# Softplus's last addition as an accumulating transfer issued by GpSimd, in a two-layer metaformer kernel

## The chip, the cores and the metric

The kernel runs on one core of a Trainium2 chip. The metric is the device time of one execution in microseconds. The time before is 26,376.83 us, the median of three runs that lie between 26,376.42 and 26,384.82.

## The reference

Input and output are 8 images of 128 x 128 tokens with 96 channels. Layer 0 mixes tokens with a filter in the Fourier domain and then applies a feed-forward block in 8-bit floats. Layer 1, which takes most of the time and holds the change, mixes tokens with a selective scan over 16,384 tokens in both directions:

```python
xc = silu(depthwise_conv3x3(xc) + conv_b)            # 192 channels
delta = jax.nn.softplus(dts + dt_projs_bias)          # step size of each channel and token
dA = jnp.exp(delta[..., None] * As)                   # 16 states for each channel
h = dA * h + (delta * u)[..., None] * Bt[:, :, None, :]
y = jnp.sum(h * Ct[:, :, None, :], axis=-1)
out = (y_forward + y_backward + skip) * silu(z) @ W_out.T
```

The kernel computes Softplus from the absolute value and the positive part of its argument a: with e = exp(-|a|) and w = 1 + e it takes log(w), corrects it for the digits of e that were lost in the sum, and adds max(a, 0).

## The kernel before

**Layer 0** fills the first 5,300 us and is not touched by the change. **The scan layer** works through 4 pairs of images. For each pair there are 32 jobs: 16 chunks of 1,024 tokens forward (`d == 0`), then the same chunks backward (`d == 1`), 128 jobs in all. A job has 12 blocks of 32 channels, and a block has 4 units of 4 states each. So a unit is one tile of 128 partitions (32 channels x 4 states) by 1,024 tokens, and a job has 48 units.

The order of the work is written out by hand. Every step is given to a `Plan` with a time in units (one unit is one scan), the plan is sorted by time, and the instructions are emitted in that order. Each engine executes its own instructions in that order, one after the other; waits come from the tiles that instructions share. A job's 48 units take about 164 us, a unit about 3.4 us.

For one unit these steps follow each other:

- SyncE loads `dlb` (step sizes spread over the states, L1209), `bt` (L1193) and `ct` (L1200) from DRAM. `dlb` and `bt` have 3 buffers, `ct` has 5.
- ScalarE makes `da`, the decay, in PSUM (L1235, two buffers).
- TensorE spreads `du` = delta x u over the states into `dub` in PSUM (L1222, `spread`, one buffer, once a block).
- VectorE multiplies `bt` by `dub` into `hp` (L1252, two units at a time) and scans in place (L1287). In some forward blocks GpSimd makes one of these products from `dus`, ScalarE's copy of `dub` (L1271).
- ScalarE keeps the last state for the next chunk (L1296).
- GpSimd multiplies the scanned states by `ct` into `hc` (L1303, three buffers).
- TensorE sums `hc` over the states into `y` (L1312).

Backward jobs also multiply by the gate (`yo`, L1368, GpSimd) and run the output projection (`po`, L1442 and L1446, TensorE) and the feed-forward block in steps laid between the units (`finish_steps`). Forward jobs have the taps of the 3 x 3 convolution on TensorE instead (`pv`, L1035).

**Softplus** is made one job ahead, in `prepare_steps`, three times a job: one chain for each of three tiles of 128 channels, in the order tile 0, tile 2, tile 1, called the first, second and third chain here. A chain runs: TensorE projects (`pd`, L1116); ScalarE takes the absolute value into `e` (L1125) and the positive part into `rl` (L1126), then exp (L1129), 1 + e into `w` (L1133) and log (L1136); VectorE computes what was lost (L1139); GpSimd subtracts it from `w` (L1144), adds `rl` to `w` (L1147) and multiplies `w` by `u` into `du` (L1154); SyncE stores `w` to `dld` in DRAM (L1150), from where `dlb` is loaded in the next job. `e`, `rl` and `w` have one buffer each. The planned times of the GpSimd and SyncE steps in a chain are set here:

```python
PREP = tuple(
    {
        "delta": (a0, a1), "exp": e, "onep": e + 0.2, "lost": e + 1.5, "log": e + 2.2,
        "sub": s0, "add": s1, "mul": m, "store": s1 + 1.1,
    }
    for a0, a1, e, s0, s1, m in (
        (12.2, 13.2, 16.2, 20.3, 21.3, 24.3),
        (24.2, 25.2, 28.2, 32.3, 33.3, 36.3),
        (37.2, 38.2, 41.2, 45.3, 48.3, 49.3),
    )
)
```

In the first two chains the addition is planned 3 units before the product with `u`, in the third chain 1 unit before it. The third chain's addition and product fall at the start of the job that follows.

Of the kernel before, what the change touches and what calls it, by code (L numbers as in the profile page):

```python
# [14 lines left out]
ALU = mybir.AluOpType  # L15
# [886 lines left out]
def scan_layer(tc, p, x2d, xcd, zsd, ud, yfd, dld, bcd, out):  # L902
# [7 lines left out]
    nc = tc.nc  # L910
# [3 lines left out]
    with ExitStack() as ctx:  # L914
# [87 lines left out]
        def halves():  # L1002
            return [(i, slice(i * HALF, (i + 1) * HALF)) for i in range(2)]

        def kind(t):
            return 0 if t < 2 else 1
# [74 lines left out]
        def prepare_steps(plan, bp, d, c, k, at0):  # L1081


            k.u, k.du = [None] * 3, [None] * 3

            def load(t):
                k.u[t] = w1.tile([128, TC], F32, tag=f"u{t}", name="u")
                nc.sync.dma_start(k.u[t], ud[bp % 2, t, :, c * TC : (c + 1) * TC])

            def project(i, hs):  # L1090
                def f():
                    if i == 0:
                        k.bc = w1.tile([NX, TC], F32, tag="bc", name="bc")
                    px = ps1.tile([NX, HALF], F32, tag="pp", name="px")
                    for t in range(3):
                        nc.tensor.matmul(  # L1096
                            px, xpw[:, d, t, :], k.u[t][:, hs], start=(t == 0), stop=(t == 2)
                        )
                    k.px = px

                return f

            def projected(hs):
                nc.scalar.copy(k.bc[:, hs], k.px)

            def store_bc():
                nc.sync.dma_start(bcd[k.s], k.bc[0 : 4 * NST])


            def delta(t, st, i, hs):  # L1110
                def f():
                    if i == 0:
                        st["e"] = w1.tile([128, TC], F32, tag="e", name="e")
                        st["r"] = w1.tile([128, TC], F32, tag="rl", name="rl")
                    pd = ps1.tile([128, HALF], F32, tag="pp", name="pd")
                    nc.tensor.matmul(  # L1116
                        pd, dtw[4 * NST : NX, d, t, :], k.bc[4 * NST : NX, hs], start=True, stop=True
                    )
                    st["pd"] = pd

                return f

            def parts(t, st, hs):
                bias = dtb[:, d, kind(t) : kind(t) + 1]
                nc.scalar.activation(st["e"][:, hs], st["pd"], AF.Abs, bias=bias)  # L1125
                nc.scalar.activation(st["r"][:, hs], st["pd"], AF.Relu, bias=bias)  # L1126

            def exp(st):
                nc.scalar.activation(st["e"], st["e"], AF.Exp, scale=-1.0)  # L1129

            def onep(st):
                st["w"] = w1.tile([128, TC], F32, tag="w", name="w")
                nc.scalar.activation(st["w"], st["e"], AF.Copy, bias=1.0)  # L1133

            def log(st):
                nc.scalar.activation(st["w"], st["w"], AF.Ln)  # L1136

            def lost(st):
                nc.vector.scalar_tensor_tensor(  # L1139
                    st["e"], st["w"], -1.0, st["e"], ALU.add, ALU.subtract  # L1140
                )

            def sub(st):
                nc.gpsimd.tensor_tensor(st["w"], st["w"], st["e"], ALU.subtract)  # L1144

            def add(st):
                nc.gpsimd.tensor_tensor(st["w"], st["w"], st["r"], ALU.add)  # L1147

            def store(t, st):
                nc.sync.dma_start(dld[k.s, t], st["w"])  # L1150

            def mul(t, st):
                k.du[t] = w1.tile([128, TC], F32, tag=f"du{t}", name="du")
                nc.gpsimd.tensor_tensor(k.du[t], st["w"], k.u[t], ALU.mult)  # L1154

            for t, at in ((0, 0.4), (1, 3.2), (2, 4.2)):
                plan(at0 + at, lambda t=t: load(t))
            for i, hs in halves():
                plan(at0 + 9.2 + 1.3 * i, project(i, hs))
                plan(at0 + 10.2 + 1.1 * i, lambda hs=hs: projected(hs))  # L1160
            plan(at0 + 12, store_bc)
            for t, at in ((0, PREP[0]), (2, PREP[1]), (1, PREP[2])):
                st = {}
                for i, hs in halves():
                    plan(at0 + at["delta"][i], delta(t, st, i, hs))
                    plan(at0 + at["delta"][i] + 0.6, lambda t=t, st=st, hs=hs: parts(t, st, hs))
                for what, f in (
                    ("exp", exp), ("onep", onep), ("lost", lost), ("log", log), ("sub", sub),
                    ("add", add),
                ):  # L1170
                    plan(at0 + at[what], lambda f=f, st=st: f(st))
                plan(at0 + at["mul"], lambda t=t, st=st: mul(t, st))
                plan(at0 + at["store"], lambda t=t, st=st: store(t, st))
# [640 lines left out]
```

## Time and profile before

| what | value |
|---|---|
| median of three runs | 26,376.83 us |
| the profiled execution | 26,377.52 us |
| its span, first to last instruction | 26,375.7 us |
| mean granted TensorE clock | 0.914 |
| VectorE busy | 25,019.3 us |
| GpSimd busy | 22,505.7 us |
| TensorE busy | 22,322.2 us |
| ScalarE busy | 17,618.2 us |
| SyncE's transfer queue, share of 16 engines | 41.7%, 3,496 MB |
| transfers issued by GpSimd | none |

The profile comes from one execution. A group is all instructions of one line, engine, operation and pair of tiles; it has a busy time, a mean duration, and the idle time that its engine had just before it, with the instruction that ended most of that idle time. A timeline lists one engine's instructions by start time and merges neighbours of a kind (x2, x3). In it PE is TensorE, DVE is VectorE, ACT is ScalarE, POOL is GpSimd and SP is SyncE; `<-` means written from, or, after an idle time, released by. The time of a transfer "to landing" runs from its issue to the signal that all its data are there.

### The profile page before, as it was taken

How to read it: one execution, taken by the hardware profiler on the slowest of the kernel's cores; microseconds unless marked ns; L12 is line 12 of the kernel's file. 1: busy time of each engine (PE TensorE's matmuls, PEld its weight loads, DVE VectorE, ACT ScalarE, POOL GpSimd, SP SyncE). 2: the span in 40 equal slices, each digit the busy share in tenths (PEclk: the TensorE clock that was granted, in tenths of full speed). 3: DMA queues.
4: the chain of work that ended last, by engine and by line, in shares of the span. 5: the costliest groups of instructions: out<-in, count | busy, mean ns of one | idle time of the engine just before them, and what ended most of it. 6: DMA issues, size and time to landing. Idle time of an engine off the chain costs nothing.

```text
span 26375.7 us, 272252 instructions
## 1 busy us (share of the span) xinstructions
PE 22322.2 (85%) x84560; PEld 8957.9 (34%) x84560; DVE 25019.3 (95%) x18514; ACT 17618.2 (67%) x31776; POOL 22505.7 (85%) x13815
## 2 busy tenths in 40 slices
PE   8999999889997777899977778998777788877777
PEld 6777777622222222222222222222222222212222
DVE  5888888699999999999999999999999999999999
ACT  5888887556666666666666666666666666656666
POOL 3666666489999999999999999999999999999998
PEclk9999999999998888999988889999888899988888
DMA  2333333344444444444444444444444444444443
GB/s 61 94 94 95 94 92 89 86 154 154 155 159 136 136 136 139 148 158 156 155 139 135 138 135 155 154 153 154 140 137 137 136 151 155 153 144 135 135 139 114
DMA packets 1887106, 3513.56 MB, mean 133 GB/s; under 512 B 564382, under 2 KB 999190, under 8 KB 1885626
## 3 DMA queue, kind: packets, MB, share of 16 engines
q1 hardware_dynamic: 1885652, 3496.14, 41.7%
q8 instruction: 672, 11.01, 0.2%
q14 instruction: 782, 6.41, 0.1%
HBM read 2739.32 MB, written 756.17 MB: 133 GB/s over the span
## 4 chain that ended last, share of the span: by engine, by line
DVE 41%; PE 18%; issue 15%; ACT 4%; POOL 3%; DVEq 0%; DMA 0%; POOLq 0%; ACTq 0%
DVE hp L1287 22%; DVE hp L1252 17%; PE pv L1035 6%; PE dub L1222 5%; PE y L1312 5%; POOL hc L1303 2%; DVE e L1139 2%; ACT da L1235 1%; PE y L1354 1%; PE pd L1116 1%; PE px L1096 0%; ACT pre L1049 0%; ACT L1061 0%; ACT L1060 0%; ACT ff_h L1543 0%
## 5 line engine op out<-in xcount | busy, mean ns | idle before, releaser
L1303 POOL TENSOR_TENSOR hc<-hp,ct 128x1024 f32<-128x1024 f32 x6144 | 14732.5, 2418 | 1175.4 <-DVE hp L1287 1048.3
L1287 DVE TENSOR_TENSOR_SCAN hp<-da,h,hp 128x1024 f32<-128x1024 f32 x6144 | 14143.0, 2338 | 207.3 <-ACT da L1235 49.0
L1312 PE MATMUL y<-hc,sely 128*32 128x512 f32 x24576 | 6959.0, 651 | 2061.1 <-POOL hc L1303 2045.0
L1235 ACT ACTIVATE da<-dlb,at 128x1024 f32<-128x1024 f32 x6144 | 6844.8, 1114 | 0.5 <-ACT h L1296 0.5
L1252 DVE TENSOR_TENSOR hp<-bt,dub 128x2048 f32<-128x2048 f32 (+1 forms) x3072 | 6558.2, 2135 | 13.4 <-PE dub L1222 12.9
L1222 PE MATMUL dub<-du,selx 128*128 128x512 f32 x6144 | 3800.0, 751 | 1332.0 <-DVE hp L1252 1331.7
L1296 ACT COPY h<-hp 128x1 f32<-128x1 f32 x6144 | 1159.1, 189 | 4769.7 <-DVE hp L1287 4753.4
L1035 PE MATMUL pv<-xin,cdiag 128*128 128x512 f32 x6912 | 3495.5, 625 | 113.8 <-ACT pre L1049 52.2
L1312 PEld LDWEIGHTS y<-hc,sely 128*32 128x32 f32 x24576 | 938.8, 112 | 6575.8 <-POOL hc L1303 4361.2
L1222 PEld LDWEIGHTS dub<-du,selx 128*128 128x128 f32 x6144 | 1286.0, 226 | 3478.7 <-issue 2164.0
L1035 PEld LDWEIGHTS pv<-xin,cdiag 128*128 128x128 f32 x6912 | 1174.5, 190 | 2466.2 <-issue 2066.4
L110 POOL TENSOR_SCALAR ln_v<-ln_v 128x4 f32<-128x4 f32 x768 | 199.9, 260 | 1288.0 <-DVE ln_v L106 1267.9
L1271 POOL TENSOR_TENSOR hp<-bt,dus 128x1024 f32<-128x1024 f32 x366 | 867.4, 2370 | 254.7 <-ACT dus L1264 204.4
L1049 ACT ACTIVATE pre<-pv,cbt 128x512 f32<-128x512 f32 x384 | 263.8, 687 | 1102.0 <-PE pv L1035 914.1
L1116 PE MATMUL pd<-bc,dtw 12*128 12x512 f32 x1536 | 913.4, 675 | 67.7 <-ACT rl L1126 47.0
L1144 POOL TENSOR_TENSOR w<-w,e 128x1024 f32<-128x1024 f32 x384 | 904.7, 2356 | 51.7 <-ACT w L1136 38.2
L111 POOL TENSOR_TENSOR ln_r<-ln_v,mhalf 128x4 f32<-128x4 f32 x768 | 885.7, 1153 | 64.0
L1154 POOL TENSOR_TENSOR du<-w,u 128x1024 f32<-128x1024 f32 x384 | 908.9, 2367 | 0.2
L1147 POOL TENSOR_TENSOR w<-w,rl 128x1024 f32<-128x1024 f32 x384 | 906.6, 2361 | 0.2
L1125 ACT ACTIVATE e<-pd,dtb 128x512 f32<-128x512 f32 x768 | 524.9, 683 | 549.5 <-PE pd L1116 532.9
L742 PE MATMUL ring<-xnt,win 96*128 96x512 f32 x1536 | 782.3, 617 | 70.8 <-ACT xnt L736 69.8
L1096 PE MATMUL px<-u,xpw 128*76 128x512 f32 x1536 | 717.2, 603 | 59.8 <-ACT ff_h L1536 57.5
(189 smaller groups left out, 32947.9 us busy)
## 6 DMA issues: line engine op xcount, KB each, us to landing
dlb<-dld SPq DMA_DIRECT2D x1536, 512.0 KB, 5.2
bt<-bcd SPq DMA_DIRECT2D x1024, 512.0 KB, 4.7
ct<-bcd SPq DMA_DIRECT2D x1024, 512.0 KB, 4.7
u<-ud SPq DMA_DIRECT2D x384, 512.0 KB, 5.0
dld<-w SPq DMA_DIRECT2D x384, 512.0 KB, 3.5
ud<-pre SPq DMA_DIRECT2D x192, 512.0 KB, 4.2
yf<-ud SPq DMA_DIRECT2D x768, 128.0 KB, 4.8
yfd<-yo SPq DMA_DIRECT2D x384, 256.0 KB, 7.1
```

What stands on the lines that cost most here:

```text
L1035: nc.tensor.matmul(st["pv"], cdiag[:, kind(t), j, :], st["xin"][:, r : r + HB // 2, j % 3 : j % 3 + W], start=(j == 0), stop=(j == 8),)
L1116: nc.tensor.matmul(pd, dtw[4 * NST : NX, d, t, :], k.bc[4 * NST : NX, hs], start=True, stop=True)
L1144: nc.gpsimd.tensor_tensor(st["w"], st["w"], st["e"], ALU.subtract)
L1147: nc.gpsimd.tensor_tensor(st["w"], st["w"], st["r"], ALU.add)
L1154: nc.gpsimd.tensor_tensor(k.du[t], st["w"], k.u[t], ALU.mult)
L1222: nc.tensor.matmul(blk["du"][:, hs], selx[:, blk["r"], :], k.du[blk["t"]][:, hs], start=True, stop=True,)
L1235: nc.scalar.activation(un["da"], blk["dl"], AF.Exp, scale=at[:, d, blk["kb"], j : j + 1])
L1252: nc.vector.tensor_tensor(hp[:, 0:n, :], bt[blk["b2"], j][:, 0:n, :], blk["du"].rearrange("p (o t) -> p o t", o=1).to_broadcast([128, n, TC]),
L1287: nc.vector.tensor_tensor_scan(h, da, h, un["init"], op0=ALU.mult, op1=ALU.add)
L1296: nc.scalar.copy(un["init"], un["h"][:, last : last + 1])
L1303: nc.gpsimd.tensor_tensor(un["hc"], un["h"], ct[blk["b2"], j], ALU.mult)
L1312: nc.tensor.matmul(y[q, :], sely, un["hc"][:, hs], start=False, stop=(j == NG - 1),)
```

## The change

In Softplus's step `add`, GpSimd's addition of two tiles in SBUF is replaced by a transfer that GpSimd issues. The transfer reads the tile `r` (named `rl` in the profile) and adds it to `w` in place, 128 partitions x 1,024 floats, 512 KB. It stands in the plan where the addition stood. The step runs 384 times, three for each of 128 jobs.

```diff
             def add(st):
-                nc.gpsimd.tensor_tensor(st["w"], st["w"], st["r"], ALU.add)
+                nc.gpsimd.dma_start(st["w"], st["r"], accum_op=ALU.add)
```

Against the instruction order before, the order of every engine is the same but for this instruction. The waits differ: the product with `u` (L1154, GpSimd), the store of `w` (L1150, SyncE) and the next writing of `rl` (L1126, ScalarE) wait for the transfer's landing, where they waited for GpSimd's addition. The transfer itself waits for the subtraction (L1144), as the addition did.

## Prediction

> **What bounds the kernel now.** I read the page's busy table first, then busy time by stretch, then the costliest groups, then timelines of one job. The page's first two parts:
>
> ```profile
> PE 22322.2 (85%) x84560; PEld 8957.9 (34%) x84560; DVE 25019.3 (95%) x18514; ACT 17618.2 (67%) x31776; POOL 22505.7 (85%) x13815
> ...
> DVE  5888888699999999999999999999999999999999
> ```
>
> From the seventh slice on (the scan layer, 5,300 us to the end) VectorE is the digit 9 everywhere. The busy time by stretch gives the exact share in mid-kernel:
>
> ```profile
> 10000.00:15000.00 5000.00, 4193.24 (x12052) 1236.04 (x12050) 4950.99 (x2291) 3248.28 (x5535) 4639.74 (x2365) 0.90 0.45 146
> ```
>
> VectorE works 4,951 of 5,000 us (third number with a count), GpSimd 4,640, and the DMA engines are 45% busy. So VectorE is the bound, at 99%; GpSimd has 360 us free in 5,000. Three groups of the page matter:
>
> ```profile
> L1303 POOL TENSOR_TENSOR hc<-hp,ct 128x1024 f32<-128x1024 f32 x6144 | 14732.5, 2418 | 1175.4 <-DVE hp L1287 1048.3
> L1287 DVE TENSOR_TENSOR_SCAN hp<-da,h,hp 128x1024 f32<-128x1024 f32 x6144 | 14143.0, 2338 | 207.3 <-ACT da L1235 49.0
> ...
> L1147 POOL TENSOR_TENSOR w<-w,rl 128x1024 f32<-128x1024 f32 x384 | 906.6, 2361 | 0.2
> ```
>
> The scan waited 207 us in all and never on GpSimd; GpSimd's products `hc` waited 1,048 us on the scan. The third line is the addition that the change replaces: 906.6 us, 2,361 ns each (busy and mean stand after the bar, then the idle time before). Taking work off GpSimd can therefore give VectorE almost nothing. What can go wrong is a new wait on GpSimd that reaches VectorE, so the question is how much delay each chain stands. The tightest place is the third Softplus of a job (tile 1) when the running job is a backward one. GpSimd's timeline there:
>
> ```profile
> 10073.23 2.38 POOL L1147 TENSOR_TENSOR w<-w,rl 128x1024 f32<-128x1024 f32 x1
> 10075.54 2.37 POOL L1303 TENSOR_TENSOR hc<-hp,ct 128x1024 f32<-128x1024 f32 x1
> 10077.85 2.38 POOL L1154 TENSOR_TENSOR du<-w,u 128x1024 f32<-128x1024 f32 x1
> 10080.17 2.36 POOL L1303 TENSOR_TENSOR hc<-hp,ct 128x1024 f32<-128x1024 f32 x1
> 10082.48 1.29 POOL L1368 TENSOR_TENSOR yo<-yo,zs 128x512 f32<-128x512 f32 x1
> 10083.71 4.68 POOL L1303 TENSOR_TENSOR hc<-hp,ct 128x1024 f32<-128x1024 f32 x2
> ```
>
> Only one `hc` stands between the addition and the product that needs it; all six run back to back. TensorE, same job:
>
> ```profile
> 10086.12 1.92 PE L1312 MATMUL y<-hc,sely 128*32 128x512 f32 x4 [1.60 <-POOL hc L1303]
> 10087.97 1.66 PE L1442 MATMUL po<-x,ident 128*128 128x388 f32 x2
> 10089.43 2.45 PE L1446 MATMUL po<-wo,yo 128*128 128x194 f32 x12
> 10091.80 1.05 PE L1312 MATMUL y<-hc,sely 128*32 128x512 f32 x4
> 10092.78 1.98 PE L1222 MATMUL dub<-du,selx 128*128 128x512 f32 x4
> ```
>
> and the VectorE product that reads `dub`:
>
> ```profile
> 10095.89 2.26 DVE L1252 TENSOR_TENSOR hp<-bt,dub 128x2048 f32<-128x2048 f32 x1
> ```
>
> `dub` is ready at 10,094.76 and wanted at 10,095.89: 1.1 us to spare behind an unbroken chain from the `hc` that ends at 10,086.05.
>
> **What the Trainium skill says.** "DMA: Bandwidth & Descriptors", section "SWDGE vs HWDGE vs iDMA": an accumulating transfer must be issued by GpSimd, whose cores write the descriptors in software. No transfer here is GpSimd's yet, so the trace can't confirm it. "Perfetto Trace Analysis", section "DMA Instruction — SWDGE (GPSIMD)": GpSimd is through when the descriptors are written, and the data land later; so its next products run meanwhile, and only the instruction that waits for the landing stands. "Collectives: The Full Stack", section "The bandwidth ceiling: the fold count and why AG ≠ RS ≠ AR": an add in the DMA path costs two source reads and so about half the copy rate, the add itself nothing. No run shows it yet. "SBUF — State Buffer", section "SBUF: two separate sides": a VectorE instruction on the shared port keeps GpSimd from writing descriptors. In the scan VectorE reads one operand from PSUM (`da`, `dub`) and one from SBUF, except L1139 (384 of 1.2 us), which does share: its mean is 1,393 ns against a minimum of 1,198.
>
> **The change part by part.**
>
> *Removed:* 384 additions of 2,361 ns on GpSimd = 907 us. They lie beside VectorE's work; value 0. The bounds: VectorE's port conflicts on L1139 are 384 x (1.393 - 1.198) = 75 us at most, and the additions don't meet L1139, so I take 0 and keep a few us below nothing.
>
> *Added on GpSimd:* 384 issues. Between 0 (a dispatch) and 2.36 us (as the addition) each; I take 1.0, the skill's first-byte latency for GpSimd's transfers ("DMA: Bandwidth & Descriptors", "Latency and other measured facts"). Up to 2.36 us it moves nothing else.
>
> *Added: the landing, L,* counted from where the addition began. All later readers of `w`, and the next writer of `rl`, wait for it. Built up: a 512 KB store of the same tile by SyncE lands after 3.5 us (`dld<-w`, DMA issues). The queue row (3,496 MB in 41.7% of 16 engines' 26,375.7 us) makes 512 KB 1.65 us of all engines; the second source read adds that: 5.15. The skill's first bytes (1.0 us for GpSimd, 0.6 for SyncE) add 0.4: 5.5. In the third chain SyncE has just issued a `u` and a `dlb` load (10,071.55 and 10,072.23), 3.3 us of engine time, about half of which is still open when GpSimd's transfer starts: +1.6. L = 7.1 us, an estimate. Low: 2.0 + 2 x 524,288/436e3 = 4.4 (the fit in the skill's "Anatomy of one DMA — SWDGE (gpsimd) path", two passes). High: two whole transfers of the slowest 512 KB row (`dlb<-dld`, 5.2), one after the other, + 0.4 = 10.8.
>
> *Third chain, 128 times.* The product L1154 began 4.62 us after the addition (10,077.85 - 10,073.23). It now begins at L, and everything behind it on GpSimd slips by L - 4.62: `yo` and three `hc`, then TensorE's `y`, the projection and `dub`. In 64 backward jobs 1.1 us is free, so VectorE loses L - 5.7: 1.4 us x 64 = 90 us. In 64 forward jobs TensorE is full of convolution taps and `dub` is 3.3 us early (ready 11,082.1, read 11,085.46), so loss begins at L = 7.9: 0 now.
>
> *First and second chain, 256 times.* Three `hc` lie between, the product is 9.25 us after the addition:
>
> ```profile
> 10144.97 2.36 POOL L1147 TENSOR_TENSOR w<-w,rl 128x1024 f32<-128x1024 f32 x1
> 10147.27 7.01 POOL L1303 TENSOR_TENSOR hc<-hp,ct 128x1024 f32<-128x1024 f32 x3
> 10154.22 2.37 POOL L1154 TENSOR_TENSOR du<-w,u 128x1024 f32<-128x1024 f32 x1
> ```
>
> At 7.1 nothing; without that cover it would be (7.1 - 2.4) x 256 = 1,200 us of GpSimd delay.
>
> *ScalarE:* L1126 rewrites `rl` 9.8 us after the first chain's addition began (10,154.80), 12 and more after the others. Behind it stand the decays L1235 that the scan needs. Covered until L = 9.8.
>
> *SyncE:* the store L1150 waits for the landing in place of the addition, 4.7 us longer; queued behind it are loads of `ct`, `bt`, `dlb`. Tightest: the first chain's `ct`, used 13 us or more after its issue, landing in 4.7, and issued 2.3 us after the store anyway: 10.6 us of cover. The stored `dld` is read over 18 units (3.4 us each) later.
>
> *DMA engines:* 384 x 3.3 us = 1,267 us, 45% to about 51% busy in the scan: 0.
>
> *Start:* three chains before the first scan, where VectorE waits 12.9 us for `dub` anyway: 0 to 5 us, I take 0.
>
> Sum: the profiled execution took 26,377.5 us (span 26,375.7 and 1.8 around it), 0.7 above the median of 26,376.8. 26,377 + 90 = **26,467 us**, +0.34%.
>
> **The rivals.** *The landing is hidden (not slower).* Place: the third chain's product; price 0 at L of 5.7 or less, 51 us at 6.5. For it: the build-up without collision gives 5.5, the skill's fit 4.4. Against: the two loads in flight. 26,377 to 26,428; it decides below L = 6.5. *A slow transfer.* Descriptors written slowly or a slow add, with L beyond 10.8: at L = 15, 64 x 9.3 + 64 x 7.1, and the first two chains lose too (slack behind 9.25 about 1.6 and 2.8 us: 128 x 4.1 + 128 x 2.9), together 1,950: 28,330. For it: nothing in the trace prices an accumulate. Against: the half-rate statement. *Freed GpSimd pays.* At most the 75 us of port conflicts and the 49 us of waits on `da`: 26,253; against it, GpSimd isn't what VectorE waits for. That the transfer does not do the addition is excluded by the instruction order: it stands in the addition's place on GpSimd, with the same readers.
>
> **How the numbers follow.** About 0.2% (53 us) is what a measurement of this kernel can tell from no change. Forecast (L from 6.5 to 10.8): 0.46. Hidden: 0.34. Slow transfer: 0.16. Freed GpSimd: 0.04. Faster 0.04, same 0.34, slower 0.62. Range: low 26,365 (hidden, a few us gained); high L = 10.8: 64 x 5.1 + 64 x 2.9 = 512, 26,890. The slow transfer (0.16) and most of the gain are left out.
>
> **What would show it.** Right: L1154 begins about 7 us after the issue in the third chain and stays near 9 in the others; VectorE waits 1 to 2 us on `dub` once in each backward job, nowhere in forward ones; SyncE's store waits longer; nobody waits on `rl`. Wrong: L1154 late in all three chains, or ScalarE standing at L1126 (slow transfer); or `hc` slower while descriptors are written; or no new wait at all (hidden).

## The result and the profile after

The changed kernel takes **26,988.46 us** (median of four runs, 26,981.66 to 26,989.48) against 26,380.41 us for the kernel before in the same comparison: 1.023 times, 95% interval 1.0212 to 1.0248. That is 608 us more, outside the predicted range of 26,365 to 26,890. The profiled execution took 26,981.66 us with a span of 26,979.9 us, 604.2 above the span before.

The busy table and VectorE's slices of the page:

```profile
PE 22345.6 (83%) x84560; PEld 8972.4 (33%) x84560; DVE 25043.9 (93%) x18514; ACT 17600.8 (65%) x31776; POOL 21957.1 (81%) x13815
...
DVE  5888888599999999999999999999999999999998
```

VectorE works as long as before (25,044 us against 25,019), while the span grew by 604: so 580 us of new idle time (604 - 25), and nearly all of the loss. GpSimd lost 549 us of work, not 907, mainly because the transfers' issues count 340 us (384 of 883 ns). The same stretch of mid-kernel as before:

```profile
10000.00:15000.00 5000.00, 4052.29 (x11695) 1190.61 (x11695) 4809.64 (x2224) 3139.69 (x5334) 4367.16 (x2282) 0.91 0.49 151
```

VectorE is down from 99% to 96%; every other engine does less too. Nobody has become the bound, so there must be new waits. Groups:

```profile
L1303 POOL TENSOR_TENSOR hc<-hp,ct 128x1024 f32<-128x1024 f32 x6144 | 14734.9, 2415 | 1577.9 <-DVE hp L1287 1477.2
L1287 DVE TENSOR_TENSOR_SCAN hp<-da,h,hp 128x1024 f32<-128x1024 f32 x6144 | 14148.5, 2337 | 342.8 <-ACT da L1235 183.6
...
L1252 DVE TENSOR_TENSOR hp<-bt,dub 128x2048 f32<-128x2048 f32 (+1 forms) x3072 | 6556.9, 2134 | 453.6 <-PE dub L1222 246.7
...
L1154 POOL TENSOR_TENSOR du<-w,u 128x1024 f32<-128x1024 f32 x384 | 902.0, 2349 | 585.8 <-DMA w<-rl 575.8
```

The means (2,415, 2,337, 2,349 ns) are those of before: these instructions of GpSimd and VectorE did not become slower. The new idle time stands in two places. GpSimd's product L1154 waits 576 us for the landing, in 129 of its 384 executions, so once a job. VectorE waits 343 us ahead of its scans (207 before) and 454 us ahead of its products L1252. L1252's own waits tell from whom (13.4 us in all before; total us, then how often):

```profile
  PE dub L1222: 246.7, 108
  ACT dus L1264: 184.5, 60
```

The second row is the surprise: ScalarE's copy `dus` has no share in the change. In each of the 60 cases, all in forward jobs, VectorE's product for one half of a tile `hp`, whose other half GpSimd makes from `dus`, begins 0.1 us after `dus` has ended. The transfers on the page:

```profile
q0 software_dynamic: 55296, 201.35, 3.8%
...
w<-rl POOLq DMA_DIRECT2D x384, 512.0 KB, 8.0
dld<-w SPq DMA_DIRECT2D x384, 512.0 KB, 3.0
```

The median landing is 8.0 us over the three chains, 4.5 at the least. It differs by chain. The second chain, in GpSimd's timeline:

```profile
10116.13 0.89 POOL L1147 DMA_DIRECT2D w<-rl  x1
10118.17 7.00 POOL L1303 TENSOR_TENSOR hc<-hp,ct 128x1024 f32<-128x1024 f32 x3 [1.15 <-DVE hp L1287]
10125.13 2.35 POOL L1154 TENSOR_TENSOR du<-w,u 128x1024 f32<-128x1024 f32 x1
```

No wait. The third, in a backward job:

```profile
10211.22 0.92 POOL L1147 DMA_DIRECT2D w<-rl  x1
...
10220.25 2.35 POOL L1154 TENSOR_TENSOR du<-w,u 128x1024 f32<-128x1024 f32 x1 [5.72 <-DMA w<-rl]
```

GpSimd stands 5.72 us, and the product begins 9.03 us after the issue, where 4.62 us lay between addition and product before. From the traces, the store of `w`, which leaves when the landing is seen, is issued a median of 8.1, 4.6 and 8.3 us after the transfer in the first, second and third chain. The first chain's landing is thus nearly as late as the third's (loads of `bt` and `dlb` have been issued just ahead of it), but its product begins only 9.0 us after the issue, so that GpSimd hardly ever stands for it. Split by job and block, VectorE's loss lies right behind the third chain: 394 us in the 64 forward jobs (6.2 each) and 210 us in the 64 backward jobs (3.3 each). In forward jobs VectorE waits 172 us for `dub` and 185 for `dus`; in backward jobs 134 us for `da` (27 before) and 61 for `dub`.

### The profile page after: what moved, and what is told of

Read it like the earlier page. It is cut to its first block, busy times and chain, and to the rows that moved or that the text cites. A ratio compares the mean times of both kernels' runs of the same rounds, so it can differ in the third digit from the quotient of the medians.

```text
span 26979.9 us, 272572 instructions
## 1 busy us (share of the span) xinstructions
PE 22345.6 (83%) x84560; PEld 8972.4 (33%) x84560; DVE 25043.9 (93%) x18514; ACT 17600.8 (65%) x31776; POOL 21957.1 (81%) x13815
## 4 chain that ended last, share of the span: by engine, by line
DVE 36%; PE 21%; issue 16%; ACT 6%; POOL 2%; DVEq 0%; POOLq 0%; ACTq 0%
DVE hp L1287 20%; DVE hp L1252 15%; PE pv L1035 8%; PE y L1312 6%; PE dub L1222 4%; ACT da L1235 2%; POOL hc L1303 2%; DVE e L1139 1%; PE y L1354 1%; PE po L1446 1%; ACT ln_q L1473 0%; ACT L1061 0%; ACT L1060 0%; ACT ff_h L1543 0%; ACT pre L1049 0%
## 5 line engine op out<-in xcount | busy, mean ns | idle before, releaser
L1303 POOL TENSOR_TENSOR hc<-hp,ct 128x1024 f32<-128x1024 f32 x6144 | 14734.9, 2415 | 1577.9 <-DVE hp L1287 1477.2
L1287 DVE TENSOR_TENSOR_SCAN hp<-da,h,hp 128x1024 f32<-128x1024 f32 x6144 | 14148.5, 2337 | 342.8 <-ACT da L1235 183.6
L1252 DVE TENSOR_TENSOR hp<-bt,dub 128x2048 f32<-128x2048 f32 (+1 forms) x3072 | 6556.9, 2134 | 453.6 <-PE dub L1222 246.7
L1222 PE MATMUL dub<-du,selx 128*128 128x512 f32 x6144 | 3683.7, 731 | 1469.5 <-DVE hp L1252 1469.5
L1035 PE MATMUL pv<-xin,cdiag 128*128 128x512 f32 x6912 | 3620.7, 644 | 102.5 <-ACT pre L1049 52.2
L1154 POOL TENSOR_TENSOR du<-w,u 128x1024 f32<-128x1024 f32 x384 | 902.0, 2349 | 585.8 <-DMA w<-rl 575.8
L1049 ACT ACTIVATE pre<-pv,cbt 128x512 f32<-128x512 f32 x384 | 263.8, 687 | 1527.6 <-PE pv L1035 979.4
L1144 POOL TENSOR_TENSOR w<-w,e 128x1024 f32<-128x1024 f32 x384 | 903.5, 2353 | 49.0 <-ACT w L1136 35.6
L652 ACT COPY img<-ring 128x384 f32<-128x384 f32 x512 | 422.8, 826 | 396.3 <-PE ring L647 396.1
```

The source lines that it names most:

```text
L1035: nc.tensor.matmul(st["pv"], cdiag[:, kind(t), j, :], st["xin"][:, r : r + HB // 2, j % 3 : j % 3 + W], start=(j == 0), stop=(j == 8),)
L1222: nc.tensor.matmul(blk["du"][:, hs], selx[:, blk["r"], :], k.du[blk["t"]][:, hs], start=True, stop=True,)
L1252: nc.vector.tensor_tensor(hp[:, 0:n, :], bt[blk["b2"], j][:, 0:n, :], blk["du"].rearrange("p (o t) -> p o t", o=1).to_broadcast([128, n, TC]),
L1287: nc.vector.tensor_tensor_scan(h, da, h, un["init"], op0=ALU.mult, op1=ALU.add)
L1303: nc.gpsimd.tensor_tensor(un["hc"], un["h"], ct[blk["b2"], j], ALU.mult)
```

## Experiments

**The theory.** The third chain's landing is late because SyncE's loads stand ahead of the transfer; GpSimd's whole row of work slips by 3.7 us (8.3 - 4.6); and the slip reaches VectorE by TensorE's `dub` and also by ScalarE's queue. **Rivals:** the first two chains cost something too; the transfers' traffic or the descriptor writing slows something; the add itself is slow.

### Which chain: only the third, and only the first two

The step is a transfer in some chains and GpSimd's addition in the others; `st["t"]` is the tile of the chain, 1 in the third. The first kernel is shown, the second has `!= 1`.

```diff
-                nc.gpsimd.dma_start(st["w"], st["r"], accum_op=ALU.add)
+                if st["t"] == 1:
+                    nc.gpsimd.dma_start(st["w"], st["r"], accum_op=ALU.add)
+                else:
+                    nc.gpsimd.tensor_tensor(st["w"], st["w"], st["r"], ALU.add)
```

> Only the third chain's addition is a transfer; the first two are GpSimd's additions again. Theory (the third chain's product L1154 waits for the landing, and GpSimd's delay reaches VectorE through TensorE and ScalarE): the whole loss stays, 26,960 to 27,000 us. Rival (every transfer costs, by its traffic and by the longer wait in SyncE's queue, about 604 / 384 = 1.6 us): a third of the loss, 26,580 us.

> Only the first two chains' additions are transfers. Theory: their three hc hide the landing, so no loss, 26,360 to 26,400 us. Rival (every transfer costs): two thirds of the loss, 26,780 us.

Measured: 26,989.02 us (ratio 1.0231, 1.0216 to 1.0247) with the third chain alone, and 26,375.57 us (0.9998, 0.9989 to 1.0006) with the first two. All of the loss is the third chain's; 256 of the 384 transfers are free, and bring nothing.

### Traffic or delay: the slip without any transfer

The kernel before, with 1.5 additional products on GpSimd behind the third chain's L1154; they compute `du` once more.

```diff
                 nc.gpsimd.tensor_tensor(k.du[t], st["w"], k.u[t], ALU.mult)
+                if t == 1:
+                    nc.gpsimd.tensor_tensor(k.du[t], st["w"], k.u[t], ALU.mult)
+                    nc.gpsimd.tensor_tensor(k.du[t][:, 0:HALF], st["w"][:, 0:HALF], k.u[t][:, 0:HALF], ALU.mult)
```

> No transfer at all: GpSimd's additions as before, but the third chain's product with u is done once and a half more, so that the hc behind it slip by 2.37 + 1.28 = 3.65 us, as they do behind the landing. Theory: the loss comes from that slip alone, about 6.3 us in a forward job and 3.7 in a backward one, 26,950 to 27,020 us. Rival of traffic and SyncE: none of it is here and GpSimd has room, 26,400 us. The prediction's own arithmetic (loss through dub only, 1.1 us free backward and 3.3 forward): 64 x 2.5 + 64 x 0.35, 26,560 us.

Measured: 26,995.15 us (1.0233, 1.0218 to 1.0248), 6.2 us lost in each forward job and 3.3 in each backward one, as in the changed kernel. So a delay of GpSimd's row by 3.6 us makes the whole loss, without a transfer: traffic, descriptors and DMA load are not needed for it.

### How the loss grows with the slip: half a product more

The same with the half product only, a slip of 1.3 us.

> As the run with a slip of 3.65 us, but half a product more, a slip of 1.28 us. Theory (TensorE stands, then runs its next matmuls slowly, and ScalarE passes the delay on with almost no cover in forward jobs): 1 to 2 us a forward job, about 1 a backward one, 26,480 to 26,570 us. The prediction's own arithmetic: 64 x 0.2, 26,390 us.

Measured: 26,608.19 us (1.0087, 1.007 to 1.0104), above what both expected: 2.6 us in each forward job, 1.1 in each backward one. VectorE's products wait 140 us for `dus` and 45 us for `dub`:

```profile
L1254 DVE TENSOR_TENSOR hp<-bt,dub 128x2048 f32<-128x2048 f32 (+1 forms) x3072 | 6560.0, 2135 | 190.7 <-ACT dus L1266 140.4 <-PE dub L1224 44.8 <-POOL ln_s L1465 5.5
```

By the prediction's forward cover of 3.3 us, a slip of 1.3 would cost forward jobs nothing. In the median forward job the slip has grown to 3.0 us at `dub`, still within the 3.3, and `dub` is waited for in only 3 of them. They have hardly any cover all the same, and what is short is ScalarE's.

### Who makes the landing late: the loads behind the store

The changed kernel, with the load of `u` and the load of `dlb` planned a little later, so that SyncE issues them behind the store that waits for the landing.

```diff
-            for t, at in ((0, 0.4), (1, 3.2), (2, 4.2)):
+            for t, at in ((0, 1.5), (1, 3.2), (2, 4.2)):
...
-                    plan(gb - 7, load_delta(blk))
+                    plan(gb - 6.5, load_delta(blk))
```

> The change, with SyncE's loads of u and dlb that stand just ahead of the third chain's store planned behind it, so that the transfer meets at most one load (ct). Theory: the transfer lands after about 5 us as in the second chain (4.5), the product slips by under 1 us, 26,380 to 26,500 us. Rival (an accumulate is slow by itself): the landing stays near 8 us and the time near 26,980 us.

Measured: 26,373.74 us (0.9997, 0.9988 to 1.0006), just under what was expected. From its page:

```profile
L1154 POOL TENSOR_TENSOR du<-w,u 128x1024 f32<-128x1024 f32 x384 | 903.7, 2353 | 109.8 <-DMA w<-rl 101.8
...
w<-rl POOLq DMA_DIRECT2D x384, 512.0 KB, 4.6
```

In the third chain the store now leaves 4.6 us after the transfer, as in the second, and L1154 still waits 102 us in all, about 1 us each time, with no loss on VectorE. The third landing is late because of the loads ahead of it. A load of `ct` stays ahead of the transfer here, and alone it delays nothing.

### The add itself: a plain copy

> The change with a plain copy in place of the accumulate: rl overwrites w, so Softplus lacks its logarithm part here. It prices the add in the transfer engines. Theory (the second read is about 1.1 us of the landing, the collision with SyncE's loads 3.7): the second chain lands after 3.2 us instead of 4.5, the third after about 7.3 instead of 8.2, so the product slips by 2.7 us and the time is 26,850 to 26,950 us. Rival (the accumulate makes the landing long): all chains land after about 3.5 us, no loss, 26,380 us.

```diff
-                nc.gpsimd.dma_start(st["w"], st["r"], accum_op=ALU.add)
+                nc.gpsimd.dma_start(st["w"], st["r"])
```

Measured: 26,748.93 us (1.014, 1.0119 to 1.016), less than the theory expected and far from the rival's 26,380. The store leaves 3.0 us after the issue in the second chain and 7.0 in the third. The add costs 4.6 - 3.0 = 1.6 us when nothing else is in flight, and 1.3 in the third chain; waiting behind the loads costs 3.7 to 4.0 us with or without it. Of the 608 us, 240 go with the add and about 370 stay.

### More time for the landing: the transfer earlier, or the product later

The third row of the planned times, with the addition 2 units earlier in one kernel and the product 1.8 units later in the other:

```diff
-                (37.2, 38.2, 41.2, 45.3, 48.3, 49.3),
+                (37.2, 38.2, 41.2, 45.3, 46.3, 49.3),
...
+                (37.2, 38.2, 41.2, 45.3, 48.3, 51.1),
```

> The change, with the third chain's transfer (and its store) planned 2 units earlier, so that three hc stand between it and the product, as in the other chains. Theory: the landing (8.2 us) ends before the product's turn, no loss: 26,360 to 26,400 us. Rival (traffic, SyncE's queue): nothing changes, 26,980 us.

> The change, with the third chain's product planned 1.8 units later instead, behind three hc; the transfer stays where it collides with the two loads. Theory: the landing is as late as before (8.2 us) but nobody stands for it, 26,360 to 26,400 us. Rival (traffic, SyncE's queue): 26,980 us.

Measured: 26,376.99 us (0.9997, 0.9989 to 1.0006) with the transfer early: the loss is gone. With the product late: 26,453.57 us (1.0027, 1.0017 to 1.0037), above what was expected. The landing is as late as ever (8.2 us) but almost never waited for (7.8 us in all). The loss lies in the forward jobs alone, 1.1 us each. VectorE's products in that kernel, from the list of groups:

```profile
L1252 DVE TENSOR_TENSOR hp<-bt,dub 128x2048 f32<-128x2048 f32 (+1 forms) x3072 | 6558.8, 2135 | 45.8 <-ACT dus L1264 32.9 <-PE dub L1222 12.9
```

The wait for `dub` is down to the start's 12.9 us; that for `dus` remains, and that for `da` is 87 us against 49 before. The two account for 71 of the 73 us. The moved product now stands ahead of a later `hc`, TensorE's `y` waits 78 us for it in the forward jobs, and `dub` slips by only 0.7 us, well within its cover; VectorE still waits 0.6 us for `dus`. The delay reaches VectorE through ScalarE alone here.

### TensorE's stand in forward jobs: the taps of the convolution one step ahead

The changed kernel with the first tap slot 0.3 units earlier; on TensorE a row of taps then stands ahead of one more `y` that waits for the late `hc`.

```diff
-        SLOTS = ((3.2, 16.2), (26.2, 31.1), (39.1, 43.6))
+        SLOTS = ((2.9, 16.2), (26.2, 31.1), (39.1, 43.6))
```

> The change, with the first half of the first tile's convolution taps planned 0.3 units earlier, so that in forward jobs two taps (2 us of TensorE) stand ahead of the sum y that waits for GpSimd. Theory (TensorE's standing and its slow matmuls after it make 6.3 us out of a slip of 3.6): TensorE works while it would stand, the forward loss falls to 2 to 3.5 us, backward jobs stay at 3.7: 26,740 to 26,840 us. Rival (the delay comes by another way than the taps behind y): 26,980 us.

Measured: 26,793.26 us (1.0155, 1.014 to 1.017). Forward jobs lose 3.1 us each where they lost 6.2, backward jobs, which have no taps, 3.4 as before. Half of the forward loss goes with the place of the taps alone, the landing being unchanged (8.2 us). The slip at `dub` is 1.9 us in the median forward job instead of 6.3, and VectorE waits there 7 us for `dub` in all instead of 172; what remains comes by `dus` (99 us) and `da` (94).

### Can the freed GpSimd pay? One product of VectorE more for GpSimd

One product L1252 in each job goes to GpSimd: in block 6 of forward jobs and in block 4 of backward ones. First in the kernel before, then in the changed kernel with the early transfer, then there with the backward product only.

```diff
-        SHARE = (1, 2, 3, 4, 7, 10)
+        SHARE = (1, 2, 3, 4, 6, 7, 10)
...
-                    share = SHARE if d == 0 and (bp == 0 or n > 0) else ()
+                    share = SHARE if d == 0 and (bp == 0 or n > 0) else (4,) * d
```

> The kernel before with one more product hp made by GpSimd in each job (block 6 in forward jobs, block 4 in backward ones): 1.06 us less on VectorE, 2.37 more on GpSimd, which is 93% busy. Theory: the room is just there in some jobs, 26,260 to 26,420 us; GpSimd has no freed time here.

> The third chain's transfer 2 units early, and the same products moved to GpSimd. Each job has 3 x (2.36 - 0.88) = 4.4 us freed on GpSimd for the 2.37. Theory (VectorE is the bound once no new wait reaches it): 124 x 1.06 = 131 us less than before, 26,230 to 26,300 us, and less than the same products without transfers. Rival (the products' own waits on dus cost as much): 26,380 us.

> The changed kernel with the third chain's transfer two units earlier, and GpSimd's freed time spent in backward jobs only: one product of L1252 in each backward job (block 4) goes to GpSimd, the forward share stays as it was. Theory: in the run with both shares the backward jobs gained 1.19 us each and the forward jobs lost 0.41 each; the early transfer alone gave 26,377. So 26,377 - 64 x 1.19 = 26,301: 26,280 to 26,320. Rival (the backward gain came from what the forward share shifted in the job before, and is lost with it): 26,350 to 26,390.

Measured: 26,483.17 us (1.0039, 1.0024 to 1.0054) in the kernel before, which missed what was expected; 26,321.01 us (0.9977, 0.9969 to 0.9986) with the early transfer, about half of the expected gain; **26,295.01 us** (0.9969, 0.9957 to 0.9982) with the backward product alone, as the theory expected. The last is the fastest of all, 0.31% below the kernel before and 2.6% below the changed kernel. The freed time matters: a backward job with the moved product gains 0.1 us in the kernel before, and 1.2 and 1.1 us in the two kernels with the early transfer.

The loss of the first comes mostly from one instruction. VectorE did 142 us less in L1252 (6,416 against 6,558), but L1139 grew from 535 to 766 us (a mean of 1,994 ns against 1,393). In a forward job of that kernel:

```profile
11679.38 4.67 POOL L1303 TENSOR_TENSOR hc<-hp,ct 128x1024 f32<-128x1024 f32 x2
...
11680.69 4.44 DVE L1139 SCALAR_TENSOR_TENSOR e<-w,e 128x1024 f32<-128x1024 f32 x1
```

L1139, whose least duration is 1,195 ns, stretches to 4.44 us and ends 1.1 us after GpSimd's two back-to-back products. In 59 forward jobs it takes 4.4 to 4.6 us; in the kernel before no execution takes over 2.4. The Trainium skill, "SBUF — State Buffer", section "SBUF: two separate sides", says that a VectorE instruction with two SBUF inputs and a GpSimd instruction that reads SBUF exclude each other on a shared port, each for its whole length. This agrees, and VectorE stood here through the rest of one product and the whole of the next. That GpSimd, with more work, leaves no gap there is argued, not tested. With both shares and the early transfer L1139 takes 648 us, with the backward product alone 542.

## Why the prediction was wrong, point by point

**The bound: right.** VectorE was at 99% (the digit 9 begins with the ninth slice of the page, not the seventh), and 907 us taken off GpSimd gave it nothing (the first two chains' transfers: 26,375.57).

**The issue, 1.0 us: right in size** (0.88). ScalarE, SyncE, the DMA engines and the start: right. ScalarE never stood at its next writing of `rl`: in the first chain, the tightest, it follows the landing by a median of 1.4 us. The store's delay led to no wait for `ct`, the queue of GpSimd's transfers takes 3.8% of the engines (4.8% was worked out), and the first two chains and the start cost nothing.

**The landing, 7.1 us: a term of the sum was mis-sized.** The base (3.5 + 1.65 + 0.4 = 5.5) measured 4.5, so the prediction's low figure of 4.4 was the nearest. SyncE's store, which gave the 3.5, takes 3.0 in the changed kernel, as the plain copy alone does. The second read (1.65) was right: 1.6. The collision was put at 1.6 and measured 3.7 (8.3 - 4.6). It was reckoned as half of two loads' 3.3 us. Three loads had been issued just ahead, as in a forward job of the changed kernel (SyncE's timeline, then GpSimd's):

```profile
11388.91 0.51 SPq L1200 DMA_DIRECT2D ct<-bcd  x1
11389.47 0.58 SPq L1088 DMA_DIRECT2D u<-ud  x1
11390.15 0.52 SPq L1209 DMA_DIRECT2D dlb<-dld  x1
...
11391.13 0.85 POOL L1147 DMA_DIRECT2D w<-rl  x1
```

The `ct` load stood at the same place before (issued at 10,070.99), inside a row of three merged loads. Between the transfer's issue and its landing, the data of 2.6 loads of 512 KB still move on SyncE's queue in the median third chain, and none in the second; at the prediction's own 1.65 us each that is 4.3 us of engine time, an estimate, not 1.6. The transfer's first data packet comes 4.4 us after the issue in the third chain and 1.45 us in the second. The Trainium skill, "DMA: Bandwidth & Descriptors", section "Queues, rings and completion order", says that a DMA engine goes round its queues packet by packet, which would let the transfer's first packets go early; here they don't, and the measurement decides. Why they don't was not settled. Together the slip is 3.7 us, not 2.5. With the prediction's own covers that is 64 x (3.7 - 1.1) + 64 x (3.7 - 3.3) = 192 us: 26,570 and inside its range.

**"In 64 forward jobs `dub` is 3.3 us early, so loss begins at L = 7.9: 0 now": this step failed.** It measured 6.2 us in each forward job, 394 us of the 604. Two things in it were wrong. A forward job of the changed kernel, in the timelines of GpSimd, TensorE, VectorE and ScalarE:

```profile
11399.33 2.35 POOL L1154 TENSOR_TENSOR du<-w,u 128x1024 f32<-128x1024 f32 x1 [3.79 <-DMA w<-rl]
...
11404.04 1.92 PE L1312 MATMUL y<-hc,sely 128*32 128x512 f32 x4 [4.11 <-POOL hc L1303]
11405.89 3.78 PE L1035 MATMUL pv<-xin,cdiag 128*128 128x512 f32 x4
...
11417.35 2.29 DVE L1252 TENSOR_TENSOR hp<-bt,dub 128x2048 f32<-128x2048 f32 x1 [2.98 <-PE dub L1222]
...
11422.33 0.69 ACT L1049 ACTIVATE pre<-pv,cbt 128x512 f32<-128x512 f32 x1 [8.96 <-issue]
11424.05 1.01 ACT L1264 COPY dus<-dub 128x1024 f32<-128x1024 f32 x1
...
11425.16 1.22 DVE L1252 TENSOR_TENSOR hp<-bt,dub 128x1024 f32<-128x1024 f32 x1 [3.07 <-ACT dus L1264]
```

*The slip grows on TensorE.* TensorE stands 4.11 us for the late `hc`, and then its `y` takes 1.92 us and its taps 3.78, where the same groups take 1.05 and 1.98 in the kernel before and later in this job: 2.7 us more. The busy time by stretch shows why (the clock is the third column from the right), for the 5.5 us after the stand:

```profile
11404.00:11409.50 5.50, 5.46 (x8) 1.36 (x8) 5.39 (x4) 2.22 (x3) 5.50 (x3) 0.50 0.90 317
```

and the same place in the kernel before:

```profile
11070.80:11076.00 5.20, 5.20 (x18) 1.40 (x18) 5.10 (x4) 3.15 (x5) 5.20 (x3) 1.00 0.87 298
```

The granted clock is 0.50 after the stand and 1.00 at the same place in the kernel before. The Trainium skill, "TensorE: Matmul & The Clock Gate", section "Part 1: The HAM clock gate (the "warmup" mystery)", has this: after an idle window of about 3.4 us the array runs at half its clock until it has been busy for as long. In the changed kernel all 114 rows of four `y` that follow a stand of 4 us or more run at a clock of 0.50 to 0.59 and take 1.7 to 1.9 us. Shorter stands can do it too: the `y` of 1.92 us among the prediction's TensorE lines followed a stand of 1.60 us, and with the slip of 1.3 us the four taps behind run at a low clock in about 6 of 10 forward jobs (in none before). The prediction carried the slip through TensorE one for one. In the median forward job, a slip of 3.6 us at L1154 is 4.5 behind the first `y` and 6.3 at `dub`: with a cover of 3.3 the loss is 3.0, as the 2.98 on VectorE shows.

*`dub` is not the only way to VectorE.* The taps are followed by their eviction on ScalarE, `pre` (L1049), and behind it in ScalarE's order stand `da` and the copy `dus`, from which GpSimd makes its share of the products. The same instructions in the kernel before, with both covers:

```profile
11080.28 1.88 PE L1222 MATMUL dub<-du,selx 128*128 128x512 f32 x4
11085.46 2.27 DVE L1252 TENSOR_TENSOR hp<-bt,dub 128x2048 f32<-128x2048 f32 x1
...
11087.18 0.69 ACT L1049 ACTIVATE pre<-pv,cbt 128x512 f32<-128x512 f32 x1 [2.64 <-issue]
11088.90 1.01 ACT L1264 COPY dus<-dub 128x1024 f32<-128x1024 f32 x1
...
11090.10 1.20 DVE L1252 TENSOR_TENSOR hp<-bt,dub 128x1024 f32<-128x1024 f32 x1
```

`dub` was 3.3 us early, but `dus` ended at 11,089.91 and VectorE's next product began at 11,090.10: 0.2 us of cover. So after the 2.98 us at `dub` VectorE waits another 3.07, and 6.3 - 0.2 = 6.1 us is the loss. The prediction measured the cover of one reader of the late chain, and listed ScalarE only for `rl`. The half product and the later product, where VectorE waits for `dus` though `dub` is in time, and the earlier taps, which shorten TensorE's part, agree.

**"In 64 backward jobs 1.1 us is free, so VectorE loses L - 5.7": the path holds, but the size is off and a second path is missing.** With the measured landing it gives 2.6; the jobs lost 3.3. The wait comes in pieces, and the first, the larger over all backward jobs, is again ScalarE's. In the backward job shown above, with a landing of 9.0 us:

```profile
10227.51 0.59 ACT L1517 ACTIVATE ff_xt<-pt 96x512 fp8e5<-96x512 f32 x1 [8.10 <-PE pt L1507]
10228.08 1.11 ACT L1235 ACTIVATE da<-dlb,at 128x1024 f32<-128x1024 f32 x1
...
10229.23 6.83 DVE L1287 TENSOR_TENSOR_SCAN hp<-da,h,hp 128x1024 f32<-128x1024 f32 x3 [2.00 <-ACT da L1235]
10237.19 2.29 DVE L1252 TENSOR_TENSOR hp<-bt,dub 128x2048 f32<-128x2048 f32 x1 [1.13 <-POOL hc L1303]
```

A step of the feed-forward block, `ff_xt`, waits for TensorE's `pt`, which stands behind the late `y`; the decay `da` behind it is 2.00 us late for the scan. The 1.13 us that follow are the delay of `dub` (the releaser named is what held TensorE's row): 3.13 together, near the slip of 4.4 less 1.1. The slip hardly grows on TensorE here (3.9 us at `dub` in the median backward job): the `y` ahead of the projection runs slowly in the kernel before as well.

**The rivals.** *Hidden* was the truth for two chains of three, and becomes it for the third when the loads or the transfer move. *A slow transfer* (beyond 10.8 us) did not come: at most 9.7. *Freed GpSimd pays* is right only if the freed time is spent, and it paid most where L1139 is not in the way.

## What to carry to other kernels

When a step becomes a transfer, place its issue where its landing is covered at the load of the queues *there*: the same transfer took 4.6 us alone and 8.3 behind three loads, and two units of plan made the difference between 0 and 608 us. For the cover of a late instruction, follow each engine that executes in order behind it, ScalarE's evictions and copies included, down to the bound engine; the smallest cover decides, not that of the nearest reader. And a stand on TensorE need not stay its own length: where the matmuls behind it had run at the full granted clock before, they ran at half, and 3.6 us became 6.3; where they had been slow already, it hardly grew.

## What the hardware showed that was not expected

- A transfer of GpSimd moved no data for 4.4 us (median) when three 512 KB loads of SyncE had been issued just ahead of it; alone the first packet came after 1.45 us.
- An accumulating packet (4,096 bytes) took 0.328 us in the median, a copying one 0.159; the 512 KB landed in 4.5 us and 3.0 us.
- A GpSimd issue occupies 0.88 us with the add and 0.61 without.
- A slip of 3.6 us on GpSimd became 6.3 us at TensorE's `dub` in forward jobs, with the granted clock at 0.50 in between.
- A VectorE instruction of 1.2 us took 4.4 us beside two back-to-back products of GpSimd.
